# A four-layer mixture-of-experts kernel on one core: the order of mixed slots, a branch hint, a row add and a running count

## The chip, the cores and the metric

The kernel runs on one core of a Trainium2 chip. Times are device microseconds of one execution. The profile is of one execution, taken by the hardware profiler.

## The reference

The input is x of shape (2, 1024, 256), that is 2048 tokens of D = 256 channels in float32, with one conditioning row per sample. Four layers follow, each of the form `x = x + ffn(cond(x))`:

```python
x = x + L0_ffn(L0_cond(x, c, w), ...)      # modulated linear; shared SwiGLU + top-1 of 32 experts
x = x + L1_ffn(L1_cond(x, c, mask), ...)   # masked attention with 16 heads; attention with gated experts
x = x + L2_ffn(L2_cond(x, c, ...), ...)    # shared + top-2 of 8 GELU experts; shared + top-2 of 8 SwiGLU experts
x = x + L3_ffn(L3_cond(x, c, ...), ...)    # shared + top-2 of 8; top-1 of 16 experts with capacity
```

For this change four pieces matter. In layer 0's FFN each token goes to the one expert with the largest logit. In layer 1, for the mask that these inputs have, the layer's contribution is the same row for all tokens of a sample, so that it is added to every token as a bias. Layer 2's FFN is, per token and for each of its two experts,

```python
out_e = (silu(x @ w1_e) * (x @ w3_e)) @ w2_e      # w1_e, w3_e: 256 x 1024, w2_e: 1024 x 256
```

The token's result is a weighted sum of those two, to which a shared expert is added.

## The kernel before

All tensors of the tokens lie in SBUF, once with tokens on the partitions (Xt, Ht) and once with channels on them (XT, HT). Routed experts work on slots: 128 rows, gathered through DRAM (xbuf), each slot with one expert. Weights are loaded by SP's queue into `ring`, an SBUF buffer of 20 pieces of 1024 columns, parts of which a stage holds for its own sets of weights. A load is issued when the code names it, and waits for the last reader of the columns that it overwrites; SP's queue is in order. A reader that is recorded in the code after a load waits for that load. All engines run their instructions in the order that the scheduler gives them, and the helper `_behind(k, a, b)` puts instruction a behind b on its engine.

**Layer 2's FFN** (`_layer2_ffn`, about 590 to 1062 us). There are 39 ordinary slots and two mixed ones, numbered 39 and 40. An ordinary slot takes W1, W3 and W2 of one expert, 1 MB each, from set 0 or set 1 in the ring. A mixed slot has rows of three experts, in quarters of 32 rows: rows 0 to 63 from the first, 64 to 95 from the second, 96 to 127 from the third. Its experts lie in sets 0, 1 and 2 (set 2 is XT and acc, which are free there); for the second mixed slot in sets 2, 0 and 1. `slots(ids)` at L2320 goes through them in the order 39, 0 to 29, 40, 30, and then, under a branch that is not taken here, the rest. Slot 0, which follows slot 39, loads into set 0; slot 30, which follows slot 40, loads into set 1.

`Series.slot` (L1938) runs one slot against its neighbours on PE. It fetches rows of the slot after next, calls `weights()` for the loads and `products(...)` for the generator of the slot's matmuls, turns the next slot's rows to channel-major (`turn`, ps_cm at L500), stages the first part of its own matmuls, and then calls `close()`, which stages the last part of the slot before and sends its rows out (`put`). Then come the other parts. For an ordinary slot (`_ffn_products`) the parts are fpg and fpu for the first 512 hidden channels (16 matmuls each, then Silu on ACT as fsg and the product fa on DVE at L1996), fpg and fpu for the second 512, and in close() fpo (L2000). For a mixed slot (`_mixed_products`, L2010) the parts are mpg for both halves, mpu for both halves (L2031), the four transposes of the first half (mpt, L2021, with a copy maT on DVE and one on ACT at L2023), and in close() the transposes of the second half and then 32 matmuls mpo (L2044), which read W2 of the three experts.

**Layer 0** (up to 282 us). `_route_static` (L771), called from `lead` in the first hidden block of the shared expert, turns each token's expert into a row number. From the one-hot tensor l_oh (128 partitions, 16 token tiles, 32 experts) 16 adds on DVE, each needing the one before, make running counts l_cum over the tiles (L783). Two matmuls into l_R follow: l_oh against `before` (L786), and l_cum against ones (L789), then l_cnt (L792). Ranks and bases are sums over experts on DVE. The row numbers drive 15 row scatters on POOL, with one more later, and the slots' rows `xs` are fetched after the last. 24 slots follow (`Split.slot`): each stages fpg, fpu, then fpo of the slot before, then the transposes. The loop calls `ahead` after each for the next weights. After the loop `mark_branch_hint_location('rare', ...)`, placed behind the last slot's up product (`split.up`), puts a hint for PE on the branch 'rare' (L751), which decides on rare cases, among them overfull experts. For these inputs the Else side runs, with `_layer1_one`.

**Layer 1** (`_layer1_one`, 282 to 335 us). The layer's row is worked out for both samples by small matmuls. `col` holds it with channels on the partitions; rb is its copy for the matmuls s_pbi against layer 2's W1 and W3, which give the biases that layer 2 would get from the row. bi is s_pbi's copy, half by ACT and half by DVE; s_pbt turns it, and k.l2b holds it. At the end eight adds put `col` on XT: four token blocks of 512 by two channel halves, one on DVE and seven on ACT (L1321), the last six behind ACT's bi copy. Then comes layer 2's first shared product (spg, L1716).

Of the kernel before, what the change touches and what calls it, by code (L numbers as in the profile page):

```python
# [9 lines left out]
F32 = mybir.dt.float32  # L10
# [3 lines left out]
BF16 = mybir.dt.bfloat16  # L14
AF = mybir.ActivationFunctionType
ALU = mybir.AluOpType
AX = mybir.AxisListType
# [3 lines left out]
P = 128  # L21
# [5 lines left out]
NT = N // P  # L27
TB = 512
NB = N // TB
# [50 lines left out]
def _bc(ap, axis, shape):  # L80
    return ap.unsqueeze(axis).to_broadcast(shape)
# [104 lines left out]
def _one_hot(k, pool, ixf, n, E, name, tag=None):  # L186
    oh = pool.tile([P, NT, E], F32, name=name, tag=tag or name)
    k.nc.vector.tensor_tensor(oh, _bc(k.iota[:, 0:E], 1, [P, NT, E]),
                              ixf[:, :, n:n + 1].to_broadcast([P, NT, E]), ALU.is_equal)
    return oh  # L190
# [334 lines left out]
def _layer0(k):  # L525
    nc, A, XT, HT, Xt, Ht = k.nc, k.A, k.XT, k.HT, k.Xt, k.Ht
# [3 lines left out]
    NS = E * C // T  # L530
# [32 lines left out]
    with ExitStack() as ctx:  # L563
# [100 lines left out]
        for i in range(NS):  # L664
# [10 lines left out]
            next(pre, None)  # L675

            ahead(3 * (i * T // C), slots.load)
        with k.tc.issue_after(split.up.ins):
            k.tc.mark_branch_hint_location('rare', 'LikelyTaken', [mybir.EngineType.PE])
        assert next(pre, pre) is pre and not todo  # L680
        rare = k.pre.tile([1, 1], F32, name="l0_raref")
        nc.vector.tensor_tensor(rare, k.differf[0:1, :], end[0:1, E - 1:E], ALU.add)
# [90 lines left out]
def _route_static(k, pool, keep, psum, ixf, E, C, nov, name, ref):  # L773

    nc = k.nc
    K = -(-(N - C) // P)
    oh = _one_hot(k, pool, ixf, 0, E, name + "_oh", "s_oh")
    cum = pool.tile([P, NT + 1, E], F32, name=name + "_cum", tag="s_cum")  # L780
    nc.vector.memset(cum[:, 0, :], 0.0)
    for t in range(NT):
        nc.vector.tensor_add(cum[:, t + 1, :], cum[:, t, :], oh[:, t, :])  # L783
    R = psum.tile([P, NT, E], F32, name=name + "_R", tag="mm")

    i = nc.tensor.matmul(R.rearrange("p t e -> p (t e)"), k.before,  # L786
                         oh.rearrange("p t e -> p (t e)"), start=True, stop=False)
    _behind(k, i, ref)
    nc.tensor.matmul(R.rearrange("p t e -> p (t e)"), k.ones,  # L789
                     cum[:, 0:NT, :].rearrange("p t e -> p (t e)"), start=False, stop=True)  # L790
    cnt = psum.tile([P, E], F32, name=name + "_cnt", tag="mm")
    nc.tensor.matmul(cnt, k.ones, cum[:, NT, :], start=True, stop=True)  # L792
    w = pool.tile([P, NT, E], F32, name=name + "_w", tag="rt")
    nc.vector.tensor_mul(w, oh, R)
    r = pool.tile([P, NT], F32, name=name + "_rank", tag="s_rank")
    nc.vector.tensor_reduce(r, w, AX.X, ALU.add)
    cs = pool.tile([P, E], F32, name=name + "_cs", tag="s_cs")
    nc.vector.tensor_copy(cs, cnt)
    thr = pool.tile([P, K], F32, name=name + "_thr", tag="s_thr")
    nc.vector.tensor_scalar(thr, k.iota[:, 0:K], float(P), float(C), ALU.mult, ALU.add)  # L800
    over = pool.tile([P, E, K], F32, name=name + "_over", tag="rt")
    nc.vector.tensor_tensor(over, _bc(cs, 2, [P, E, K]), _bc(thr, 1, [P, E, K]), ALU.is_gt)
    nt = pool.tile([P, E], F32, name=name + "_nt", tag="s_nt")
    nc.vector.tensor_reduce(nt, over, AX.X, ALU.add)
    end = pool.tile([P, E], F32, name=name + "_end", tag="s_end")
    nc.vector.tensor_tensor_scan(end, k.ones[:, 0:E], nt, 0.0, ALU.mult, ALU.add)
    base = pool.tile([P, E], F32, name=name + "_base", tag="s_base")
    nc.vector.tensor_sub(base, end, nt)
    w2 = pool.tile([P, NT, E], F32, name=name + "_w2", tag="rt")
    nc.vector.tensor_tensor(w2, oh, _bc(base, 1, [P, NT, E]), ALU.mult)  # L810
    b = pool.tile([P, NT], F32, name=name + "_b", tag="s_b")
    nc.vector.tensor_reduce(b, w2, AX.X, ALU.add)

    nc.vector.tensor_scalar(b, b, float(P), float((E - 1) * C), ALU.mult, ALU.add)
    e = pool.tile([P, NT], F32, name=name + "_e", tag="s_e")
    nc.vector.tensor_scalar_mul(e, ixf[:, :, 0], float(C))
    ge = pool.tile([P, NT], F32, name=name + "_ge", tag="s_ge")
    nc.vector.tensor_single_scalar(ge, r, float(C), ALU.is_ge)
    nc.vector.tensor_tensor(b, b, e, ALU.subtract)
    nc.vector.tensor_mul(b, b, ge)  # L820
    nc.vector.tensor_tensor(b, b, e, ALU.add)
    nc.vector.tensor_tensor(r, r, b, ALU.add)
    rows = keep.tile([P, NT], U32, name=name + "_rows", tag="s_rows")
    nc.vector.tensor_copy(rows, r)
    done = pool.tile([1, nov, E], F32, name=name + "_done", tag="rt")
    nc.vector.tensor_tensor(done, _bc(end[0:1, :], 1, [1, nov, E]),
                            _bc(k.iota[0:1, 0:nov], 2, [1, nov, E]), ALU.is_le)
    ef = pool.tile([1, nov], F32, name=name + "_ef", tag="s_ef")
    nc.vector.tensor_reduce(ef, done, AX.X, ALU.add)
    nc.vector.tensor_scalar_min(ef, ef, float(E - 1))  # L830
    eid = keep.tile([1, nov], I32, name=name + "_eid", tag="s_eid")
    nc.vector.tensor_copy(eid, ef)
    n = keep.tile([1, 1], I32, name=name + "_nov", tag="s_nov")
    nc.vector.tensor_copy(n, end[0:1, E - 1:E])
    return rows, eid, n, end
# [191 lines left out]
def _layer1_one(k, psum, last):  # L1027
# [17 lines left out]
    def fill(n=1):  # L1045

        nonlocal last
        for _ in range(n):
            i = next(ahead, None)
            if i is not None:  # L1050
                pe(i)
            elif last is not None:
                last = _warm(k, psum, last, 2, tag="o", bufs=2)

    with ExitStack() as ctx:
# [237 lines left out]
        nc.vector.tensor_copy(rb[:, :, 0:2], pc)  # L1293
        nc.vector.tensor_copy(col, pc)
        fill()

        W1, W3, _ = k.l2
        pbi = psum.tile([P, TB], F32, name="s_pbi", tag="mm")
# [2 lines left out]
                pe(nc.tensor.matmul(pbi[quad[g], :], rb[:, c, :], (W1, W3)[g // 2][:, c, (g % 2) * TB:(g % 2 + 1) * TB],  # L1301
                                    start=c == 0, stop=c == 1, skip_group_check=True))
        bi = pool.tile([P, TB], F32, name="s_bi")
        copied = nc.scalar.copy(bi[:, 0:256], pbi[:, 0:256])
        nc.vector.tensor_copy(bi[:, 256:TB], pbi[:, 256:TB])
        pb = psum.tile([P, 2, D], F32, name="s_pb", tag="t", bufs=2)
        for b in range(2):
            pe(nc.tensor.matmul(pb[:, b, :], ab[:, b, :], row, start=True, stop=True))
# [3 lines left out]
            pe(nc.tensor.transpose(pbt[:, j, :], bi[:, j * P:(j + 1) * P], k.ident))  # L1312
        nc.vector.tensor_copy(k.l2b, pbt.rearrange("p j (g r) -> p j g r", g=4)[:, :, :, 0:2])
        nc.scalar.copy(rows, pb)
        for g in range(NB):
            for c in range(2):
                x = XT[:, c, g * TB:(g + 1) * TB]
                if g == c == 0:
                    nc.vector.tensor_scalar_add(x, x, col[:, c, 0:1])
                else:  # L1320
                    i = nc.scalar.activation(x, x, AF.Identity, bias=col[:, c, g // 2:g // 2 + 1])  # L1321
                    if g:
                        _behind(k, i, copied)
        assert next(ahead, None) is None


# [311 lines left out]
def _behind(k, inst, ref):  # L1638

    k.tc.add_manual_dep(inst.ins, ref.ins.name,  # L1640
                        mybir.DependencyInfo(mybir.DependencyClass.NoSync,
                                             mybir.DependencyReason.SCHED_ONLY))
# [266 lines left out]
class Series:  # L1909
# [3 lines left out]

    def __init__(self, k, slots, ids):
        self.k, self.slots, self.ids = k, slots, list(ids)
        self.xT, self.last, self.old = {}, None, None
        self.fetch(0)
        self.fetch(1)
        self.turn(0)
# [15 lines left out]
            self.xT[i] = self.slots.rows(i, made)  # L1935
            self.stage(made)

    def slot(self, i, products, weights):  # L1938

        n = self.ids.index(i)  # L1940
        self.fetch(n + 2)
        p = products(self.xT.pop(i), *weights())
        self.turn(n + 1)
        self.stage(next(p))
        self.close()
        part = next(p)
        while part is not None:
            self.stage(part)
            self.part = part
            part = next(p)  # L1950
        self.old = i, p
# [300 lines left out]
def _layer2_ffn(k):  # L2252
# [64 lines left out]
    def mixed(m, *to):  # L2317
        return [_expert_load(k, mid, 3 * m + q, sets[j], E) for q, j in enumerate(to) if j is not None]

    def slots(ids):  # L2320
        series = Series(k, by, ids)
        for n, i in enumerate(ids):
            if i == NS:
                series.slot(i, _mixed_products(k, pool, psum), lambda: mixed(0, 0, 1, 2))
            elif i > NS:
                series.slot(i, _mixed_products(k, pool, psum), lambda: [ahead[0], *mixed(1, None, 0, 1)])
            else:
                series.slot(i, _ffn_products(k, pool, psum, 2), lambda: weights(i))
            if i == 8:
                ahead = mixed(1, 2)  # L2330
            if i == MOST - 1:
                with k.tc.issue_after(series.part[len(series.part) // 2].ins):
                    k.tc.mark_branch_hint_location('l2f', 'LikelyTaken', [mybir.EngineType.PE])
        series.close()
# [551 lines left out]
```

## Time and profile before

| what | value |
|---|---|
| median of 3 runs | 1409.55 us (1408.58 to 1412.58) |
| the profiled execution's own time | 1411.02 us |
| its span | 1409.3 us |
| mean granted TensorE clock | 0.992 |
| PE busy | 1364.5 us, 97% of the span |
| DVE, ACT, POOL busy | 459.5, 304.3, 272.7 us |
| DMA, all queues | 265.25 MB, mean 188 GB/s |

The page divides the span into 40 slices; PE's busy share is nine tenths or more in nearly all of them. The waits view lists, for each engine, what it waited for with the time in total, the number of times and the longest. The timeline gives runs of equal instructions of an engine with start, length and the idle time ahead of them. The windows view gives busy time, clock and DMA traffic for any stretch. What is named behind an arrow is the instruction whose end is nearest to the end of the wait, which need not be what the instruction was waiting for.

### The profile page before, as it was taken

The page shows a single profiled execution, that of the slowest core. Times are in us where ns is not written, and L with a number is a line of the kernel's source. Part 1 is how long each engine was busy: PE and PEld are TensorE (multiplying, and loading weights), DVE is VectorE, ACT ScalarE, POOL GpSimd, SP SyncE. Part 2 cuts the span into 40 slices and gives each one's busy share as a digit, 9 for nine tenths or more (in the row PEclk, how much of TensorE's full clock was granted, in tenths as well). Part 3 has the DMA queues.
Part 4 walks back from the last instruction along what each step waited for, and adds up shares of the span by engine and source line. Part 5 has one row for each costly group of instructions (what it writes and reads, how often), then busy time and mean ns, then how long its engine had stood idle before and what let it go on. Part 6 is the DMA issues. An engine that isn't in the chain of part 4 may idle for free. (4 is left out here: it accounts for less than half of the span.)

```text
span 1409.3 us, 23114 instructions
## 1 busy us (share of the span) xinstructions
PE 1364.5 (97%) x8431; PEld 958.7 (68%) x8431; DVE 459.5 (33%) x1528; ACT 304.3 (22%) x640; POOL 272.7 (19%) x308
## 2 busy tenths in 40 slices
PE   9999999998999999999899999999999999998997
PEld 4544444654657876555599999999966557875675
DVE  4523322324413444511211111111114423458432
ACT  3212221234112112211111111111112212127121
POOL 0410001300432430053000000010000074430441
PEclk9999999999999999999999999999999999999899
DMA  9879992943312852092284456266447347748670
GB/s 313 308 238 342 357 368 84 302 90 135 113 53 80 249 188 81 1 334 70 81 309 157 152 197 222 78 209 225 149 156 256 122 158 233 244 148 280 206 230 16
DMA packets 185423, 265.25 MB, mean 188 GB/s; under 512 B 16759, under 2 KB 134655, under 8 KB 185296
## 3 DMA queue, kind: packets, MB, share of 16 engines
q1 hardware_dynamic: 163984, 221.65, 48.4%
q0 software_dynamic: 13744, 36.63, 7.3%
q10 hardware_dynamic: 7568, 5.34, 1.2%
q8 instruction: 71, 1.16, 0.3%
q14 instruction: 56, 0.46, 0.1%
HBM read 283.67 MB, written 46.82 MB: 235 GB/s over the span
## 5 line engine op out<-in xcount | busy, mean ns | idle before, releaser
L402 POOL DMA_INDIRECT tbuf<-ys,sdst x105 | 103.3, 984 | 467.0 <-ACT ys L2003 295.4
L1669 PE MATMUL spo<-ring,sa 128*128 128x256 f32 x704 | 164.9, 380 | 0.6 <-DVE sa L1697 0.4
L1669 PEld LDWEIGHTS spo<-ring,sa 128*128 128x128 f32 x704 | 132.8, 190 | 45.8 <-issue 28.9
L1697 DVE TENSOR_TENSOR sa<-ssg,spu 128x512 f32<-128x512 f32 x88 | 60.4, 686 | 241.5 <-PE spu L1684 232.8
L1996 DVE TENSOR_TENSOR fa<-fsg,fpu 128x512 f32<-128x512 f32 x62 | 42.6, 688 | 286.0 <-PE fpu L1991 286.0
L1991 PE MATMUL fpu<-xsT,ring 128*128 128x128 f32 x992 | 122.8, 278 | 5.3 <-SPq L2338 2.9
L1991 PE MATMUL fpg<-xsT,ring 128*128 128x128 f32 x992 | 121.1, 276 | 0.9 <-ACT maT L2023 0.9
L1991 PEld LDWEIGHTS fpu<-xsT,ring 128*128 128x128 f32 x992 | 117.4, 195 | 5.7 <-issue 5.7
L1991 PEld LDWEIGHTS fpg<-xsT,ring 128*128 128x128 f32 x992 | 117.9, 192 | 3.4 <-ACT maT L2023 1.1
L2000 PE MATMUL fpo<-ring,fa 128*128 128x256 f32 x496 | 112.3, 380 | 0.0
L1693 ACT ACTIVATE ssg<-spg 128x512 f32<-128x512 f32 x88 | 52.5, 597 | 267.8 <-PE spg L1684 261.5
L2000 PEld LDWEIGHTS fpo<-ring,fa 128*128 128x128 f32 x496 | 92.1, 191 | 11.8 <-issue 0.8
L1684 PE MATMUL spg<-HT,ring 128*128 128x512 f32 x192 | 92.1, 594 | 3.1 <-issue 2.4
L1684 PE MATMUL spu<-HT,ring 128*128 128x512 f32 x192 | 90.2, 593 | 0.0
L1967 PE MATMUL cph<-xsT,ring 128*128 128x128 f32 x576 | 77.5, 278 | 6.0 <-DMA ring<-in_L_r 4.3
L1684 PE MATMUL spg<-XT,ring 128*128 128x512 f32 x160 | 75.6, 594 | 1.3 <-PEq L2214 1.2
L1967 PEld LDWEIGHTS cph<-xsT,ring 128*128 128x128 f32 x576 | 70.1, 192 | 9.1 <-DVE sn L1893 3.7
L1684 PE MATMUL spu<-XT,ring 128*128 128x512 f32 x160 | 75.4, 593 | 0.0
L1974 PE MATMUL cpo<-ring,ch 128*128 128x256 f32 x288 | 73.8, 380 | 0.0
L1995 ACT ACTIVATE fsg<-fpg 128x512 f32<-128x512 f32 x62 | 37.0, 597 | 139.9 <-PE fpg L1991 139.9
L1684 PEld LDWEIGHTS spu<-HT,ring 128*128 128x128 f32 x192 | 36.3, 190 | 44.4 <-issue 43.9
L1889 DVE COPY xsT<-ps_cm 128x256 f32<-128x256 f32 x129 | 53.8, 417 | 31.2 <-PE ps_cm L500 31.1
(675 smaller groups left out, 1770.5 us busy)
## 6 DMA issues: line engine op xcount, KB each, us to landing
ring<-in_L_w SPq DMA_DIRECT2D x105, 1024.0 KB
ring<-in_L_r SPq DMA_DIRECT2D x72, 512.0 KB
ring<-in_L_r SPq DMA_DIRECT2D x144, 256.0 KB
xs<-xbuf SPq DMA_DIRECT2D x129, 129.0 KB
ring<-in_L_W SPq DMA_DIRECT2D x32, 512.0 KB
yt<-tbuf SPq DMA_DIRECT2D x48, 256.0 KB
XT<-in_L_r SPq DMA_DIRECT2D x16, 512.0 KB
HT<-in_L_r SPq DMA_DIRECT2D x8, 512.0 KB
```

The costliest lines, as they stand in the source:

```text
L402: i = k.nc.gpsimd.indirect_dma_start(out=self.ap, out_offset=bass.IndirectOffsetOnAxis(ap=idx, axis=0), in_=rows, in_offset=None, **end)
L1669: mm = nc.tensor.matmul(po[g // 2][:, g % 2, :], a[:, g * P:(g + 1) * P], W2[:, f, :], start=f == 0 and g % 2 == 0, stop=f == nf - 1, skip ...
L1684: mm = nc.tensor.matmul(ps, W[:, c, f * P:(f + 1) * P], X[:, c, cols], start=c == 0, stop=c == 1)
L1693: k.silu = nc.scalar.activation(sg, pg, AF.Silu)
L1697: mul = nc.vector.tensor_mul(a, sg, pu)
L1889: turned = nc.vector.tensor_copy(xT, _channel_major(k, self.psum, xs, made=made))
L1967: made = [nc.tensor.matmul(ph[:, f, :], R1[:, c, f * P:(f + 1) * P], xT[:, c, :], start=c == 0, stop=c == 1) for f in range(2) for c in ra ...
L1974: made = [nc.tensor.matmul(po, h[:, f, :], R2[:, f, :], start=f == 0, stop=f == 1) for f in range(2)]
L1991: made = [nc.tensor.matmul(ps[:, j, :], W[:, c, (f0 + j) * P:(f0 + j + 1) * P], xT[:, c, :], start=c == 0, stop=c == 1) for ps, W in ((pg, ...
L1995: nc.scalar.activation(sg, pg, AF.Silu)
L1996: nc.vector.tensor_mul(a[:, f0:f0 + 4, :], sg, pu)
L2000: made = [nc.tensor.matmul(po, a[:, f, :], W2[:, f, :], start=f == 0, stop=f == 4 * nh - 1) for f in range(4 * nh)]
```

## The change

There are four parts.

1. The branch hint of layer 0 is placed behind the up product of slot NS − 3 = 21, not of the last, 23.
2. `_route_static` has its one-hot tensor with the tiles innermost, with a zero column ahead of each expert's 16 tiles. One scan over 32 x 17 elements, `state = row * state + M`, with row 0 at each expert's start and 1 elsewhere, makes the running counts. `row` lies in the last two token tiles of Xr as bfloat16. The matmuls read the same tensors in the new order (l_R is expert by tile), and the two sums over experts read with a stride.
3. `_layer1_one` adds `col` to XT ahead of the s_pbi matmuls, five of the eight adds on DVE and three (the second channel half of blocks 0 to 2) on ACT, each engine's own in order; the bi copies come behind them.
4. A slot can be marked `soon`, which both mixed slots are. The slot after it then calls `close()` ahead of its own first part, not behind it. `weights()` and `turn` come ahead of that, as before.

```diff
--- before.py
+++ after.py
@@ -675,8 +675,9 @@
             next(pre, None)
 
             ahead(3 * (i * T // C), slots.load)
-        with k.tc.issue_after(split.up.ins):
-            k.tc.mark_branch_hint_location('rare', 'LikelyTaken', [mybir.EngineType.PE])
+            if i == NS - 3:
+                with k.tc.issue_after(split.up.ins):
+                    k.tc.mark_branch_hint_location('rare', 'LikelyTaken', [mybir.EngineType.PE])
         assert next(pre, pre) is pre and not todo
         rare = k.pre.tile([1, 1], F32, name="l0_raref")
         nc.vector.tensor_tensor(rare, k.differf[0:1, :], end[0:1, E - 1:E], ALU.add)
@@ -776,24 +777,28 @@
 
     nc = k.nc
     K = -(-(N - C) // P)
-    oh = _one_hot(k, pool, ixf, 0, E, name + "_oh", "s_oh")
-    cum = pool.tile([P, NT + 1, E], F32, name=name + "_cum", tag="s_cum")
-    nc.vector.memset(cum[:, 0, :], 0.0)
-    for t in range(NT):
-        nc.vector.tensor_add(cum[:, t + 1, :], cum[:, t, :], oh[:, t, :])
-    R = psum.tile([P, NT, E], F32, name=name + "_R", tag="mm")
-
-    i = nc.tensor.matmul(R.rearrange("p t e -> p (t e)"), k.before,
-                         oh.rearrange("p t e -> p (t e)"), start=True, stop=False)
+    M = pool.tile([P, E, NT + 1], F32, name=name + "_oh", tag="s_oh")
+    row = k.Xr[:, NT - 2:, :].rearrange("p t d -> p (t d)").bitcast(BF16)[:, 0:E * (NT + 1)]
+    row = row.rearrange("p (e t) -> p e t", e=E)
+    nc.vector.memset(row, 1.0)
+    nc.vector.memset(row[:, :, 0:1], 0.0)
+    nc.vector.memset(M[:, :, 0:1], 0.0)
+    oh = M[:, :, 1:]
+    nc.vector.tensor_tensor(oh, _bc(k.iota[:, 0:E], 2, [P, E, NT]), _bc(ixf[:, :, 0], 1, [P, E, NT]), ALU.is_equal)
+    cum = pool.tile([P, E, NT + 1], F32, name=name + "_cum", tag="s_cum")
+    nc.vector.tensor_tensor_scan(cum.rearrange("p e t -> p (e t)"), row.rearrange("p e t -> p (e t)"),
+                                 M.rearrange("p e t -> p (e t)"), 0.0, ALU.mult, ALU.add)
+    R = psum.tile([P, E, NT], F32, name=name + "_R", tag="mm")
+
+    i = nc.tensor.matmul(R, k.before, oh, start=True, stop=False)
     _behind(k, i, ref)
-    nc.tensor.matmul(R.rearrange("p t e -> p (t e)"), k.ones,
-                     cum[:, 0:NT, :].rearrange("p t e -> p (t e)"), start=False, stop=True)
+    nc.tensor.matmul(R, k.ones, cum[:, :, 0:NT], start=False, stop=True)
     cnt = psum.tile([P, E], F32, name=name + "_cnt", tag="mm")
-    nc.tensor.matmul(cnt, k.ones, cum[:, NT, :], start=True, stop=True)
-    w = pool.tile([P, NT, E], F32, name=name + "_w", tag="rt")
+    nc.tensor.matmul(cnt, k.ones, cum[:, :, NT], start=True, stop=True)
+    w = pool.tile([P, E, NT], F32, name=name + "_w", tag="rt")
     nc.vector.tensor_mul(w, oh, R)
     r = pool.tile([P, NT], F32, name=name + "_rank", tag="s_rank")
-    nc.vector.tensor_reduce(r, w, AX.X, ALU.add)
+    nc.vector.tensor_reduce(r, w.rearrange("p e t -> p t e"), AX.X, ALU.add)
     cs = pool.tile([P, E], F32, name=name + "_cs", tag="s_cs")
     nc.vector.tensor_copy(cs, cnt)
     thr = pool.tile([P, K], F32, name=name + "_thr", tag="s_thr")
@@ -806,10 +811,10 @@
     nc.vector.tensor_tensor_scan(end, k.ones[:, 0:E], nt, 0.0, ALU.mult, ALU.add)
     base = pool.tile([P, E], F32, name=name + "_base", tag="s_base")
     nc.vector.tensor_sub(base, end, nt)
-    w2 = pool.tile([P, NT, E], F32, name=name + "_w2", tag="rt")
-    nc.vector.tensor_tensor(w2, oh, _bc(base, 1, [P, NT, E]), ALU.mult)
+    w2 = pool.tile([P, E, NT], F32, name=name + "_w2", tag="rt")
+    nc.vector.tensor_tensor(w2, oh, _bc(base, 2, [P, E, NT]), ALU.mult)
     b = pool.tile([P, NT], F32, name=name + "_b", tag="s_b")
-    nc.vector.tensor_reduce(b, w2, AX.X, ALU.add)
+    nc.vector.tensor_reduce(b, w2.rearrange("p e t -> p t e"), AX.X, ALU.add)
 
     nc.vector.tensor_scalar(b, b, float(P), float((E - 1) * C), ALU.mult, ALU.add)
     e = pool.tile([P, NT], F32, name=name + "_e", tag="s_e")
@@ -1293,6 +1298,17 @@
         nc.vector.tensor_copy(rb[:, :, 0:2], pc)
         nc.vector.tensor_copy(col, pc)
         fill()
+        added = {}
+        for g in range(NB):
+            for c in range(2):
+                x, by, one = XT[:, c, g * TB:(g + 1) * TB], col[:, c, g // 2:g // 2 + 1], c == 1 and g < 3
+                if one:
+                    i = nc.scalar.activation(x, x, AF.Identity, bias=by)
+                else:
+                    i = nc.vector.tensor_scalar_add(x, x, by)
+                if one in added:
+                    _behind(k, i, added[one])
+                added[one] = i
 
         W1, W3, _ = k.l2
         pbi = psum.tile([P, TB], F32, name="s_pbi", tag="mm")
@@ -1301,8 +1317,8 @@
                 pe(nc.tensor.matmul(pbi[quad[g], :], rb[:, c, :], (W1, W3)[g // 2][:, c, (g % 2) * TB:(g % 2 + 1) * TB],
                                     start=c == 0, stop=c == 1, skip_group_check=True))
         bi = pool.tile([P, TB], F32, name="s_bi")
-        copied = nc.scalar.copy(bi[:, 0:256], pbi[:, 0:256])
-        nc.vector.tensor_copy(bi[:, 256:TB], pbi[:, 256:TB])
+        _behind(k, nc.scalar.copy(bi[:, 0:256], pbi[:, 0:256]), added[True])
+        _behind(k, nc.vector.tensor_copy(bi[:, 256:TB], pbi[:, 256:TB]), added[False])
         pb = psum.tile([P, 2, D], F32, name="s_pb", tag="t", bufs=2)
         for b in range(2):
             pe(nc.tensor.matmul(pb[:, b, :], ab[:, b, :], row, start=True, stop=True))
@@ -1312,15 +1328,6 @@
             pe(nc.tensor.transpose(pbt[:, j, :], bi[:, j * P:(j + 1) * P], k.ident))
         nc.vector.tensor_copy(k.l2b, pbt.rearrange("p j (g r) -> p j g r", g=4)[:, :, :, 0:2])
         nc.scalar.copy(rows, pb)
-        for g in range(NB):
-            for c in range(2):
-                x = XT[:, c, g * TB:(g + 1) * TB]
-                if g == c == 0:
-                    nc.vector.tensor_scalar_add(x, x, col[:, c, 0:1])
-                else:
-                    i = nc.scalar.activation(x, x, AF.Identity, bias=col[:, c, g // 2:g // 2 + 1])
-                    if g:
-                        _behind(k, i, copied)
         assert next(ahead, None) is None
 
 
@@ -1913,7 +1920,7 @@
 
     def __init__(self, k, slots, ids):
         self.k, self.slots, self.ids = k, slots, list(ids)
-        self.xT, self.last, self.old = {}, None, None
+        self.xT, self.last, self.old, self.soon = {}, None, None, False
         self.fetch(0)
         self.fetch(1)
         self.turn(0)
@@ -1935,14 +1942,17 @@
             self.xT[i] = self.slots.rows(i, made)
             self.stage(made)
 
-    def slot(self, i, products, weights):
+    def slot(self, i, products, weights, soon=False):
 
         n = self.ids.index(i)
         self.fetch(n + 2)
         p = products(self.xT.pop(i), *weights())
         self.turn(n + 1)
+        if self.soon:
+            self.close()
         self.stage(next(p))
         self.close()
+        self.soon = soon
         part = next(p)
         while part is not None:
             self.stage(part)
@@ -2321,9 +2331,10 @@
         series = Series(k, by, ids)
         for n, i in enumerate(ids):
             if i == NS:
-                series.slot(i, _mixed_products(k, pool, psum), lambda: mixed(0, 0, 1, 2))
+                series.slot(i, _mixed_products(k, pool, psum), lambda: mixed(0, 0, 1, 2), True)
             elif i > NS:
-                series.slot(i, _mixed_products(k, pool, psum), lambda: [ahead[0], *mixed(1, None, 0, 1)])
+                series.slot(i, _mixed_products(k, pool, psum), lambda: [ahead[0], *mixed(1, None, 0, 1)],
+                            True)
             else:
                 series.slot(i, _ffn_products(k, pool, psum, 2), lambda: weights(i))
             if i == 8:
```

## The prediction

> **What bounds the kernel.** I read the page first. The span is 1409.3 us, the profiled execution's own time 1411.02 us (1.7 us lie around the span), the median of the runs 1409.55 us. I add my terms to 1411.02 and then take off 1.47 us to come to the median.
>
> ```profile
> span 1409.3 us, 23114 instructions
> PE 1364.5 (97%) x8431; PEld 958.7 (68%) x8431; DVE 459.5 (33%) x1528; ACT 304.3 (22%) x640; POOL 272.7 (19%) x308
> ```
>
> PE is busy for 97%: only about 45 us of the span are without a matmul. So an edit is worth what it does to PE's idle time, to the number of PE's instructions (unchanged here) and to PE's clock. The second view is therefore the list of PE's waits (us in total, times, longest):
>
> ```profile
> PE fpu L1991 <- SPq L2338: 2.9, 1, 2.9
> PE spg L1716 <- ACT XT L1321: 2.7, 1, 2.7
> PE spg L1684 <- issue: 2.4, 1, 2.4
> PE fpu L1991 <- DMA ring<-in_L_w: 2.4, 1, 2.4
> PE l_R L789 <- DVE l_cum L783: 1.1, 1, 1.1
> PE fpg L1991 <- ACT maT L2023: 0.9, 1, 0.9
> PE mpo L2044 <- DVE fa L1996: 0.5, 1, 0.5
> ```
>
> All four edits meet here: lines 1, 4, 6 and 7 are the slots that follow the two mixed slots of layer 2, line 2 is layer 1's row add, line 3 the branch behind layer 0, line 5 layer 0's counts. If everything vanished, 12.9 us would go.
>
> **Mixed slots, the decisive part.** The third view is PE's timeline behind mixed slot 0 (start, us, instruction, in brackets the idle time before it):
>
> ```profile
> 698.88 0.66 PE L2021 MATMUL mpt<-ident,ma 128*128 128x128 f32 x4
> 699.38 0.38 PE L500 MATMUL ps_cm<-ident,xs 128*128 128x128 f32 x2
> 700.65 2.02 PE L1991 MATMUL fpg<-xsT,ring 128*128 128x128 f32 x16 [0.89 <-ACT maT L2023]
> 705.06 2.02 PE L1991 MATMUL fpu<-xsT,ring 128*128 128x128 f32 x16 [2.39 <-DMA ring<-in_L_w]
> 706.92 0.60 PE L2021 MATMUL mpt<-ident,ma 128*128 128x128 f32 x4
> 708.01 0.42 PE L2044 MATMUL mpo<-ring,maT 128*32 128x256 f32 x3 [0.49 <-DVE fa L1996]
> ```
>
> SP's queue issues six loads of 1 MB in this time: slot 0's W1 at 695.54, W3 at 698.97, W2 at 699.57, then slot 1's W1 at 700.10 and W3 at 700.80. The sixth, slot 1's W2, waits 9.2 us for mpo. From 700 to 712 us the DMA engines move 4.2 MB at a mean of 350 GB/s, so that the loads land one behind the other: W1 lets fpg start at 700.65, W3 lets fpu start at 705.06. The same ring columns hold the mixed slot's W2 and slot 0's W2, and weights() is called ahead of close(), in both kernels. In the instruction list the first mpo therefore waits for slot 0's W2 load, in both. The DVE copy that its bracket goes by had been over since 700.16 us; what ended the 0.49 us can only be that landing, at about 708.0. Before, fpg and fpu of slot 0 fill the time until then. After, mpt and mpo stand ahead of them: mpt is ready, mpo is not, and fpg, whose W1 is there at 700.65, queues behind it on PE, which is in order.
>
> So PE ends its second mpt at about 700.3 and idles until 708.0: 7.7 us in place of 0.89 + 2.39 + 0.49 = 3.77. mpo takes 3.6 us (to 711.60). Before, fpg of the second half starts at 711.60; after, fpg and fpu of the first half must still run, 3.7 us (such a pair goes from 1054.30 to 1057.97 in slot 30). **+3.7 us.** If W2 lands as early as W3 did (705.1), it is +0.8; later than 708.0 it can't be.
>
> Mixed slot 1 is alike: W3 and W2 of slot 30 are issued at 1040.27 and 1040.9, and mpo reads the columns that this W2 fills. Before, fpu starts at 1045.53 and fpo at 1057.97. DMA traffic ends in the slice 1047 to 1048, so W2 lands at about 1048.0 (not before W3, 1045.5; not after mpo's start, 1050.06). After: idle from about 1041.6 to 1048.0, mpo 3.6, two pairs 7.3, so fpo at 1058.9 at full clock.
>
> **The clock.** The windows view (PE, PEld, DVE, ACT, POOL busy, then the granted clock, DMA share, GB/s):
>
> ```profile
> 1043.00:1044.00 1.00, 0.00 (x0) 0.00 (x0) 0.00 (x0) 0.27 (x1) 0.00 (x0) 1.00 1.07 442
> 1045.00:1046.00 1.00, 0.47 (x2) 0.51 (x3) 0.00 (x0) 0.00 (x0) 0.00 (x0) 0.50 1.09 381
> 1047.00:1048.00 1.00, 1.00 (x6) 1.00 (x6) 0.00 (x0) 0.00 (x0) 0.00 (x0) 0.50 0.60 188
> 1051.00:1052.00 1.00, 1.00 (x20) 0.54 (x16) 0.00 (x0) 0.00 (x0) 0.00 (x0) 0.79 0.00 0
> ```
>
> An idle time of 2.95 us is followed here by 6.8 us at a granted 0.50 (1044.4 to 1051.2): fpu takes 3.75 us in place of 1.95. Idle times of 2.39, 2.45 and 2.75 us (the lines above) were not followed by any, one of 2.15 us ahead of 1310.85 was: length alone does not decide. The three other spells, from 1290 to 1318 us, last 3.3, 3.7 and 6.8 us. With 7.7 and 6.4 us of idle time I expect a spell behind both, of 3.3 to 6.8 us, part of which falls into the idle time itself; work lost is half of it, 1.7 to 3.4 us, and I take 2.6 each. With it slot 0 is late by 3.7 + 2.6 = **6.3 us** (0.8 to 7.1), and slot 30's fpo starts at 1061.5 in place of 1057.97: **+3.5 us** (with W2 at 1045.5 and no loss −1.6; with 1050.06 and 3.4 us lost +6.4). Both together: +9.8.
>
> [...]
>
> **The row add of layer 1.** PE's first matmul of layer 2 waits 2.75 us (332.80 to 335.55) for the last of seven ACT adds (0.64 us each, the last four 332.94 to 335.50). The adds now stand ahead of the bi copies, while PE still does pbi (until 330.87): three on ACT from 328.87, 3 x 0.64, to 330.8, and five on DVE. The only DVE add took 0.49 us and overlaps its neighbours; at 0.43 to 0.49 each they end at 331.1 to 331.3. ACT's bi copy started at 330.97 and DVE's at 331.37, so neither is pushed, and pbt is on time. The wait shrinks to what PE needs for its start, 0 to 0.4 us: **−2.5 us** (0 to −2.75; 0 if DVE's adds push bi and pbt by as much as they save). What is late next is the l2b copy at 333.03, not needed by spg.
>
> **Layer 0's counts.** 16 DVE adds (36.26 to 40.1) become one scan of 128x544. The nearest rows are the scans 128x32, 0.224 us, and 128x136, 0.442 us: 2.1 ns per element, so 1.3 us, to 37.6. PE's first l_R ends at 37.70; its waits of 1.11 us ahead of L789 and 0.41 us in the transposes that stand in between go, or part of them. The two reduces read with a stride now, at 0.36 in place of 0.27 us for 128x128, so 0.2 to 0.4 us each for four times the elements is given back on the way to the row numbers; the memsets lie in idle time. The later chain (15 row scatters on POOL, the last at 74.93, SP's fetch of xs at 77.70) ends in a wait of 0.86 us for xs at 79.99, where what PE gained can be lost again if that chain starts no earlier. **−0.8 us** (+0.8 to −1.5).
>
> **The branch hint.** PE waits 2.45 us behind the branch (236.53, "issue"). On DVE, which has no hint, the same branch costs 3.0 us; on PE in layer 2, with a hint 5.1 us ahead of its branch, 0.63 us. Here the hint runs at 226.4, 6.8 us ahead of the branch at 233.2, and helps little. After, it is about 13 us earlier, at about 213 us, where DMA traffic falls from over 90% to quiet. Either it helps now, −1.8 us, or lead was not what it lacked, 0. Nearer lies 0, since 5.1 us were enough elsewhere: **−0.3 us**.
>
> **The sum**: +9.8 − 2.5 − 0.8 − 0.3 = +6.2; 1411.0 + 6.2 = 1417.2, less 1.47 is **1415.7 us**. By the lower bounds of all terms −0.8 − 2.75 − 1.5 − 1.8 = −6.9, 1402.7; by the upper +13.5 + 0 + 0.8 + 0 = +14.3, 1423.8.
>
> **Rivals.** (B) *The wait is there, but cheap*: W2 lands nearly with W3, or the clock holds. Without any loss of clock the slots are 3.7 + 0.9 = +4.6, less 3.6 for the other edits: 1410.5; with W2 landing early as well, down to 1402.7. For it: 2.75 us idle at 332.80 left the clock alone. Against: the new idle times are twice as long.
> (C), on the other side: *mpo doesn't wait for the next slot's W2.* mpt and mpo fill the time in which PE waits for W1 and W3: 0.6 + 3.6 = 4.2 us of work, against 3.77 us of waiting behind slot 0, all of which goes; behind slot 30 the 2.95 us go and the clock never falls (2.9 us). That is −9.6 −3.6: 1396.3 us. It decides if mpo starts by about 701 us. For it: the waits view names DVE for the 0.49 us, not a DMA. Against: the DVE copy was long done.
> (D) *Edits that do nothing*: hint without effect, counts swallowed at xs: 1416.8, within the forecast's own range.
>
> **Chances.** Forecast with D, 1411 to 1422: 0.60. B, 1402 to 1411: 0.24. C: 0.13. Above 1422: 0.03. The range 1402 to 1422 leaves out 0.16. A measurement of this kernel can tell about 0.3% (4.2 us) from no change: faster (under 1405.3) C and 0.05 of B, 0.18; the same (to 1413.8) 0.26; slower 0.56.
>
> **What will show it.** PE's waits after: an entry of 5 to 8 us ahead of mpo, twice, and none ahead of fpu; windows at 0.50 behind each. spg L1716's wait under 0.5 us. No wait at l_R. The first spg behind the branch: 2.45 or 0.6 us. Wrong if mpo starts within 2 us of its mpt, if the clock stays at 1.00 behind 7 us of idle time, or if DVE's adds end later than 331.4.

## The result, and the profile after

The changed kernel takes 1414.72 us at the median of 13 runs (1412.53 to 1418.48), the kernel before 1409.55 us at the median of as many beside it (1405.56 to 1413.83). The ratio is 1.0036, with a 95% interval of 1.0023 to 1.0049: the change makes the kernel slower by 3 to 7 us. The forecast was +6.2 us, 1415.7 us. The profiled execution took 1413.27 us, its span is 1411.6 us.

The page of the changed kernel, first two lines, and then its list of PE's waits (engine, line, what ended the wait; us in total, times, longest):

```profile
span 1411.6 us, 23099 instructions
...
PE 1364.6 (97%) x8431; PEld 955.5 (68%) x8431; DVE 461.1 (33%) x1519; ACT 302.3 (21%) x636; POOL 273.3 (19%) x308
```

```profile
PE mpo L2054 <- DMA ring<-in_L_w: 6.7, 1, 6.7
PE mpo L2054 <- SPq L2349: 6.6, 1, 6.6
...
PE spg L1691 <- issue: 2.2, 1, 2.2
...
PE ps_cm L500 <- DMA xs<-xbuf: 0.7, 2, 0.5
```

PE has as many instructions as before and is busy as long. Of the seven waits that were shown of the kernel before, those ahead of fpg and fpu (0.9, 2.4, 2.9 us), of l_R (1.1) and of layer 2's first spg (2.7) are gone, but for 0.17 us at l_R and 0.43 us at spg. In their place stand two waits ahead of mpo, 6.7 and 6.6 us. The branch's wait, 2.2 us, has stayed.

PE's timeline of the changed kernel behind mixed slot 0 (lines of mpo left out):

```profile
694.80 0.66 PE L2031 MATMUL mpt<-ident,ma 128*128 128x128 f32 x4
695.30 0.38 PE L500 MATMUL ps_cm<-ident,xs 128*128 128x128 f32 x2
695.79 0.66 PE L2031 MATMUL mpt<-ident,ma 128*128 128x128 f32 x4
703.16 0.65 PE L2054 MATMUL mpo<-ring,maT 128*32 128x256 f32 x3 [6.71 <-DMA ring<-in_L_w]
...
709.46 2.05 PE L2001 MATMUL fpg<-xsT,ring 128*128 128x128 f32 x16
711.34 1.95 PE L2001 MATMUL fpu<-xsT,ring 128*128 128x128 f32 x16
713.13 1.95 PE L2001 MATMUL fpg<-xsT,ring 128*128 128x128 f32 x16
```

The first and last of these have their counterparts before in the line at 698.88, which the prediction shows, and in this one:

```profile
711.60 2.05 PE L1991 MATMUL fpg<-xsT,ring 128*128 128x128 f32 x16
```

mpt starts 4.08 us earlier than before (694.80 for 698.88), fpg of slot 0's second half 1.53 us later (713.13 for 711.60): the slot has lost 5.61 us. One mpo takes 0.65 us here and 0.42 us before. The windows view says why (the clock is the third figure from the end):

```profile
697.00:698.00 1.00, 0.00 (x0) 0.00 (x0) 0.00 (x0) 0.32 (x1) 0.00 (x0) 1.00 1.01 414
699.00:700.00 1.00, 0.00 (x0) 0.00 (x0) 0.00 (x0) 0.00 (x0) 0.00 (x0) 0.50 0.98 349
...
706.00:707.00 1.00, 1.00 (x13) 0.47 (x9) 0.00 (x0) 0.00 (x0) 0.00 (x0) 0.50 1.07 418
...
709.00:710.00 1.00, 1.00 (x16) 0.59 (x9) 0.00 (x0) 0.34 (x1) 0.00 (x0) 1.00 0.01 3
```

PE is idle from 696.45; the granted clock falls at about 698.5 and comes back at about 708.7, when mpo is nearly done. Behind mixed slot 1 it is the same: idle until 1050.34, the clock at 0.50 from about 1046.6 to 1053.4, fpo of slot 30 at 1062.66 in place of 1057.97. The lines of mpo and fpo after, and that of fpo before:

```profile
1050.34 0.63 PE L2054 MATMUL mpo<-ring,maT 128*32 128x256 f32 x1 [6.60 <-SPq L2349]
1062.66 3.62 PE L2010 MATMUL fpo<-ring,fa 128*128 128x256 f32 x16
```

```profile
1057.97 3.62 PE L2000 MATMUL fpo<-ring,fa 128*128 128x256 f32 x16
```

By landmarks on PE in the two traces: the slots of layer 0 start 1.36 us earlier (first fpg 79.56 for 80.92), the first spg behind the branch 1.63 us earlier (234.90 for 236.53), layer 2's first spg 3.78 us earlier (331.77 for 335.55), slot 30's fpo 4.69 us later. The two lines of spg, before and after:

```profile
335.55 1.98 PE L1716 MATMUL spg<-XT,ring 128*128 128x512 f32 x4 [2.75 <-ACT XT L1321]
```

```profile
331.77 1.95 PE L1723 MATMUL spg<-XT,ring 128*128 128x512 f32 x4 [0.43 <-PE s_pbt L1328]
```

At the end of the span 2.3 us are left. Between slot 30's fpo and that end no line of the change runs; before idled 1.5 us more there (ahead of ps_bk and cph, above all) and had one spell of 3.4 us at 0.50 more. I take this for chance of single executions: over 13 runs each the difference is 5.2 us.

### The profile page after: what moved, and what is told of

It is laid out like the page before. It is cut to its first block, busy times and chain, and to the rows that moved or that the text cites. A ratio compares the mean times of both kernels' runs of the same rounds, so it can differ in the third digit from the quotient of the medians.

```text
span 1411.6 us, 23099 instructions
## 1 busy us (share of the span) xinstructions
PE 1364.6 (97%) x8431; PEld 955.5 (68%) x8431; DVE 461.1 (33%) x1519; ACT 302.3 (21%) x636; POOL 273.3 (19%) x308
```

## Experiments

**The mixed slots alone, and the rest alone.** All times are set against the kernel before on the same chip. e1 is the kernel before, with part 4 of the change and nothing else:

```diff
         self.turn(n + 1)
+        if self.soon:
+            self.close()
         self.stage(next(p))
```

> The kernel before with part 4 alone (close() of a mixed slot ahead of the next slot's first part, still behind its weights()). Theory (mpo waits for the next slot's W2 load, and the idle time halves the clock): in the trace after, slot 0's second fpg is late by 5.6 us more than its mpt, and slot 30's fpo by 3.3 us more, so +8.9 us against before, a ratio of 1.0063 (1.0045 to 1.0080); two idle times of 6 to 7.5 us ahead of mpo. Rival (the two slots cost little, and the 5.2 us of the change come from another part or from layer 3's spells of the clock): under +4 us, ratio below 1.003.

Measured: 1418.58 us for 1408.17, ratio 1.0085 (1.0071 to 1.0099). The two waits ahead of mpo are 6.71 and 6.25 us, and the first spg behind the slots is reached 7.96 us later in the trace (1070.19 for 1062.23). The interval says 10 to 14 us, more than the trace and than the 8.9 us that I expected, and the ratio lies a little above the expected range; the rival is out. Where the 8.9 us fell short is taken up below, in point 3 of why the prediction was right.

e2 is the changed kernel without part 4; its core:

```diff
-        if self.soon:
-            self.close()
```

> The changed kernel without part 4. Theory: the other three parts give in full what the trace after shows up to layer 2's first spg, 331.77 in place of 335.55, so -3.8 us against before, ratio 0.9973 (0.996 to 0.9985); waits ahead of fpu and mpo as before. Rival (what PE gains early is taken back at later waits for DMA, as cph's): 0 to -1.5 us, ratio 0.999 to 1.000.

Measured: 1403.84 us for 1408.17, ratio 0.9967 (0.9956 to 0.9978). The other three parts keep what they gain. Against this the whole change is 1.0036 / 0.9967 = 1.0069, some 9.7 us (7 to 12 by the two intervals), slower through part 4 alone: the forecast's term was +9.8.

**What mpo waits for.** If it waits for the next slot's W2 because that load is recorded ahead of it, then closing ahead of the loads must take the wait away. e3 is the changed kernel with this edit:

```diff
-        p = products(self.xT.pop(i), *weights())
-        self.turn(n + 1)
         if self.soon:
             self.close()
+        p = products(self.xT.pop(i), *weights())
+        self.turn(n + 1)
```

> The changed kernel, with close() ahead of weights() for a slot behind a mixed one, so that the next slot's W2 load waits for mpo and not mpo for it. Theory: PE waits under 1 us ahead of mpo, fpg and fpu find W1 and W3 landed, the clock stays at 1.00 in both places: -3.8 -9.2 = -13 us against before, up to 3 us less if slot 1's loads, now behind mpo, come late; ratio 0.991 (0.990 to 0.9945). Rival (the loads themselves are the limit there, whatever the order: 5 MB at 350 to 400 GB/s): PE waits the same 4 to 7 us somewhere in slot 0 or slot 1, -3.8 us or less, ratio 0.997 or above.

Measured: 1398.81 us for 1408.17, ratio 0.9942 (0.9928 to 0.9955), faster than both kernels, at the small end of what was expected. From PE's timeline of e3 (32 mpo and a ps_cm between the first two lines are left out):

```profile
695.45 0.66 PE L2031 MATMUL mpt<-ident,ma 128*128 128x128 f32 x4 [0.31 <-DVE ma L2048]
...
699.90 1.95 PE L2001 MATMUL fpg<-xsT,ring 128*128 128x128 f32 x16
701.69 1.95 PE L2001 MATMUL fpu<-xsT,ring 128*128 128x128 f32 x16
...
708.40 2.02 PE L2001 MATMUL fpg<-xsT,ring 128*128 128x128 f32 x16 [0.97 <-DVE sn L1900]
711.01 2.02 PE L2001 MATMUL fpu<-xsT,ring 128*128 128x128 f32 x16 [0.59 <-DMA ring<-in_L_w]
```

mpo waits for nothing in both places, slot 0 finds its weights, and no slice shows a clock under 1.00 there. What is left are 0.97 and 0.59 us ahead of slot 1's products at 708.40 and 711.01. Now SP's queue holds slot 0's W2 until mpo is done (699.73), and slot 1's loads stand behind it. The wait ahead of the first spg behind slot 30 has grown too, to 1.46 us from 0.63 before.

In both kernels mpo reads what the *next* slot's W2 load has put into the columns, and in e3 what the mixed slot's own load did. For the drawn inputs this is the same matrix: by the reference the experts of this layer get 315, 532, 766, 431, 654, 388, 375 and 635 rows, so that slot 39's first expert is expert 0, as slot 0's is, and slot 40 has no third expert: its rows 96 to 127 are empty. For other counts it need not be so; then only an order as in e3, W2's load behind close(), has mpo read its own weights. Behind slot 39 PE waited 6.7 us for a second copy of weights that were there, behind slot 40 6.6 us for weights of rows that are empty.

e9 is e3, with slot 0's W1 and W3, and then slot 1's, issued ahead of close(). weights() of the slot behind a mixed one is a generator there; its first step issues those four loads, its second slot 0's W2:

```diff
+        w = weights()
         if self.soon:
+            early = next(w)
             self.close()
-        p = products(self.xT.pop(i), *weights())
+            w = early + next(w)
+        p = products(self.xT.pop(i), *w)
```

> As e3, but of slot 0's loads only W2 comes behind close(), and slot 1's W1 and W3 are issued ahead of it, so that they need not wait for mpo on SP's queue. Theory (what e3 still loses at 708.4 and 711.0, 0.97 and 0.59 us, is the three loads that queue behind the one that waits for mpo): both waits go, 1.5 us less than e3: ratio to before 0.993 (0.9915 to 0.9945), no idle time over 0.4 us from 694 to 720. Rival (six loads in 12 us are the limit of the DMA engines, so that a wait comes back at slot 0's fpu or fpo or slot 1's fpu): as e3, 0.994 to 0.9955.

Measured: 1412.92 us where the kernel before took 1423.7 us (another chip), ratio 0.9926 (0.9910 to 0.9941), the fastest version. The timeline shows no idle time from 697 to 724 us: both waits are gone. Between e3 and e9 the intervals overlap, so that in time the further gain is not shown, only in the trace.

**The clock.** Does the idle time halve it, or the DMA traffic of 350 to 420 GB/s that goes on meanwhile? e4 is the changed kernel with 14 filling matmuls, e5 with 30:

```diff
         made = turn(1)
+        w = psum.tile([P, F], F32, name="fill", tag="mm")
+        made += [nc.tensor.matmul(w.rearrange("p (j q) -> p j q", q=P), k.ident16, _bc(k.ident16, 1, [P, 4, P]),
+                                  start=True, stop=True, skip_group_check=True) for _ in range(14)]
```

> The changed kernel with 14 bf16 matmuls of 128x512 (0.43 us each, into a tile that nobody reads) between the second mpt and mpo, which keep PE busy while it waits for W2. Theory (the idle time itself halves the clock): mpo starts as late as before, but at 1.00; 2.7 us less behind slot 39 and 1.7 us less behind slot 40 than in the changed kernel, so 1410.3 us, ratio to before 1.0005 (0.9985 to 1.002). Rival (the half clock comes from the DMA traffic or from elsewhere): the spells at 0.50 stay, ratio 1.0035 to 1.005.

Measured: 1414.12 us for 1408.17, ratio 1.0045 (1.0032 to 1.0059). It told nothing: a filler takes some 0.21 us and not 0.43 when they run one behind another (30 take 6.64 us in e5; 0.43 us is the distance from start to start of the float32 matmuls of this width in before, as mpu's at 695.31 and 695.74), so 3.73 and 3.47 us of idle time stayed ahead of mpo and the clock still fell, to 0.50 from about 702.7 on, for 3.4 us behind slot 39 and 6.8 us behind slot 40.

> As e4, with 30 of the filling matmuls in place of 14: in e4 the 14 took 3.2 us, 3.7 and 3.5 us of idle time were left, and the clock still fell to 0.50, so that e4 could not tell the theories apart. At 0.21 us each 30 take 6.5 us and reach up to the landing of W2. Theory (idle time halves the clock): no slice under 0.9 from 694 to 710 and from 1040 to 1058, and 2.7 + 1.7 us less than the changed kernel's 1414.7: 1410.3, ratio to before 1.0005 to 1.002. Rival (the DMA traffic halves it): the spells stay, ratio 1.0035 to 1.005.

Measured: 1409.85 us for 1408.98, ratio 1.0008 (0.9998 to 1.0017). The fillers of e5 and its windows:

```profile
696.75 6.64 PE L2054 MATMUL fill<-ident 128*128 128x512 bf16 x30
703.64 0.42 PE L2057 MATMUL mpo<-ring,maT 128*32 128x256 f32 x3 [0.26 <-DMA ring<-in_L_w]
```

```profile
700.00:702.00 2.00, 2.00 (x11) 0.94 (x10) 0.00 (x0) 0.00 (x0) 0.00 (x0) 1.00 1.08 371
702.00:704.00 2.00, 1.74 (x15) 0.75 (x17) 0.00 (x0) 0.00 (x0) 0.00 (x0) 1.00 1.08 390
704.00:706.00 2.00, 2.00 (x44) 1.42 (x38) 0.00 (x0) 0.00 (x0) 0.00 (x0) 1.00 1.03 412
```

mpo starts as late as in the changed kernel (8.4 us behind its first mpt in both), under the same traffic, but at 0.42 us and a clock of 1.00. In this kernel the idle time of 6.7 and 6.6 us is what brings the clock to 0.50, and the halved clock was (1.0036 − 1.0008) x 1409 = 3.9 us of the change's cost (some 2 to 6 by the two intervals), 4.4 expected. The wait itself is the rest.

**The other three parts.** e6, e7 and e8 are the kernel before with part 3, part 2 and part 1 of the change, each alone, as in the diff of the change.

> The kernel before with part 3 alone. Theory: the wait ahead of layer 2's first spg falls from 2.75 to 0.43 us as in the trace after, and nothing takes it back: -2.3 us, ratio 0.9984 (0.997 to 0.9995). Rival (cph's waits for weights in layer 2's conditioning take it back): ratio 0.9995 to 1.0005.

Measured: 1406.85 us for 1408.98, ratio 0.9983 (0.9973 to 0.9994). The wait ahead of layer 2's first spg is 0.43 us.

> The kernel before with part 2 alone. Theory: the waits of 1.11 and 0.41 us at l_R and ps_tm go, xs's wait stays at 0.5 to 0.9 us, so the first slot's fpg starts 1.3 us earlier: -1.3 us, ratio 0.9991 (0.998 to 1.000). Rival (the wait for xs swallows it): first fpg of the slots as before within 0.4 us, ratio 0.9997 to 1.0005.

Measured: 1406.89 us for 1408.98, ratio 0.9989 (0.9978 to 1.0000). The waits for xs at the first slot are 0.60 and 0.63 us in place of 0.86, and the first fpg starts at 80.28 for 80.92. So here about half of the gain was swallowed, in the trace of the whole change nothing (its waits for xs are 0.74 us in all); the time can't tell. Single traces scatter here: on the chips of e1 to e8 the first fpg starts at 80.92, 80.91, 80.63 and 80.29 with the old counts (before, e1, e6, e8), at 79.56, 79.40, 79.37, 79.55, 79.59 and 80.28 with the new (the changed kernel, e2 to e5, e7), 1.1 us earlier in the mean.

> The kernel before with part 1 alone. Traces with the hint in its old place show the branch on PE at 3147 and 3092 ns, with the new place 2807, 3102, 2547 and 2537 ns. Theory: the place changes the branch by chance only or by 0.4 us at most: -0.3 us, ratio 0.9998 (0.999 to 1.0005). Rival (two slots earlier is what it lacked): 0.6 us of idle time ahead of the first spg, -1.8 us, ratio 0.9987.

Measured: 1408.93 us for 1408.98, ratio 1.0002 (0.9991 to 1.0013). The branch on PE takes 2957 ns.

e10 is the kernel before without the hint; in e11 the two lines stand in the loop, under `if i == NS // 2`:

```diff
-        with k.tc.issue_after(split.up.ins):
-            k.tc.mark_branch_hint_location('rare', 'LikelyTaken', [mybir.EngineType.PE])
```

> The kernel before without the branch hint of layer 0. Theory (the hint in either place leaves the branch at 2.5 to 3.1 us, so it does little): branch on PE 2.5 to 3.3 us, idle 1.8 to 2.6 us, ratio 1.000 (0.999 to 1.001). Rival (the hint does part of the fetch and the branch would be longer without it): branch above 3.5 us, ratio above 1.0005.

> The kernel before with the hint behind slot 12's up product, some 75 us ahead of the branch. One look at the branch on PE. Theory (lead is not what the hint lacks): 2.5 to 3.3 us, idle 1.8 to 2.6 us. Rival (the fetch needs longer under full DMA traffic): idle 0.6 us.

Measured: e10 1426.0 us for 1423.7, ratio 1.0018 (1.0006 to 1.0030); e11 1423.61 us in its one run. The branch as an instruction of PE's queue, in e10 and in e11 (ns three times, start in us):

```profile
L749 PEldq COMPARE_BRANCH  x1: 4082/4082/4082, 234.2 to 234.2; - x1
```

```profile
L752 PEldq COMPARE_BRANCH  x1: 2952/2952/2952, 234.6 to 234.6; - x1
```

Here my theory fell in half: the hint does something. Without it the branch takes 4.08 us and PE idles 3.38 us, about 1.1 us more than with it. The time says 2.6 us (0.9 to 4.3); in e10's trace the 3.38 us are followed by 6.8 us at a clock of 0.50, which may be the rest. But with the hint in the old place the branch took 3147, 3092, 2642 and 2667 ns in four traces, in the new place 2807, 3102, 2547, 2537, 2942, 2957 and 3067 ns in seven, and 2952 ns with a lead of 75 us. Lead is not what it lacks. What makes up the remaining 2.5 to 3.1 us, where layer 2's hinted branch cost 0.63 us of idle time in before, stays open.

## Why the prediction was right

1. *mpo must wait, since weights() stays ahead of close().* Right, shown by e3. The idle times were forecast at 7.7 and 6.4 us and are 6.7 and 6.6, the first 1.0 us too long. W2 landed at 703.2 in place of 703.9 (708.0 less the 4.1 us by which all is earlier); why it came 0.7 us sooner is not shown.
2. *The clock.* That both idle times would halve it was right, shown by e5; that the losses come so near the 2.6 us forecast for each is in part luck. The spells were put at 3.3 to 6.8 us; they last 10.2 us behind slot 39, of which 4.7 fall into the idle time, and 6.8 behind slot 40. (The spell of before ran from 1044.6 to 1051.4, not from 1044.4 to 1051.2, and the two short ones both last 3.4 us; the sums don't change.) Behind slot 39 mpo took 703.16 to 709.46, 6.3 us for 3.6: 2.7 us. Behind slot 40 it took 1050.34 to 1055.42, some 1.5 us too long. e5 gives 3.9 us for both in place of 5.2.
3. *Slots 0 and 30 late by 6.3 and 3.5 us.* 5.6 and 3.3 in the trace. In time 9.7 us by difference, 10 to 14 us by e1, for 9.8. The 3.3 are low, and so near the forecast because both start from the same trace of before, which lost 2.9 us to its own spell behind slot 40. From slot 40's first mpt to slot 30's fpo the seven traces without part 4 (before, e2, e6 to e8, e10, e11) take 15.9 to 17.8 us, before 17.84; the changed kernel and e1 take 21.1 and 22.0. From slot 39's first mpt to slot 0's second fpg the seven take 11.7 to 13.2 us, the two 18.3 and 17.1. By these means part 4 costs 5.4 and 4.8 us, 10.2 together, which fits both times.
4. *The row add, −2.5 us.* In the trace 3.78 − 1.63 = 2.15 us, in time −2.4 us. DVE's five adds took 2.07 us (2.2 to 2.4 reckoned), ACT's three 1.95, and they pushed neither copy.
5. *The counts, −0.8 us.* The scan took 1.29 us for 1.3. In the trace of the whole change the slots start 1.36 us earlier, in e7 0.64, in the mean of the traces above 1.1. I had missed that the one-hot write takes 1.09 us in the new layout in place of 0.69 (it ends at 37.17 and PE waits 0.17 us for it), and put the strided reduce at 0.2 to 0.4 us more: it is 1.03 for 0.69.
6. *The hint, −0.3 us.* Nothing that can be measured, e8.

The sum of the trace's terms up to slot 30 is −1.36 − 0.28 − 2.15 + 5.61 + 3.26 = +5.1 us against +6.2, and in time +5.2 (the stretches between gained 0.4 us more, hence the 4.69). Rival C (mpo doesn't wait) would have been 1396.3 us, 13 less than before; e3 and e9, in which it really doesn't, are 8 and 10 us below before by their ratios. Rival B (a wait without loss of clock) would have been 1410.5 us, 1.0 more than before; e5, which makes it so, is 1.1 above. Both had the wrong condition; B's price was right, C's some 3 to 5 us too low.

## What to carry to other kernels

When a step is moved ahead of another, look at which loads were recorded ahead of it, not only at its own inputs: a load into columns that it reads becomes its input, even where it brings the same data (6.7 and 6.6 us of waiting here, none in e3). A step that had other work in front of it may have been waiting all along, and the trace shows this only as half a microsecond (0.49 us ahead of mpo in before). And the idle times of 6.7 and 6.6 us on PE cost more than themselves here: the clock, at 0.50 behind both, added 1.5 to 2.7 us to each.

## What was not expected of the hardware

The clock fell 2.0 us after PE had gone idle behind slot 39 (696.45 to about 698.5) and about 2.9 us after it had behind slot 40 (1043.7 to 1046.6); in the kernel before an idle time of 2.75 us did nothing and one of 2.15 us did. The same wait need not have the same price. The one of 2.8 to 2.95 us ahead of slot 30's fpu is followed by 6.8 us at 0.50 in before and e8, by 3.4 us in e6 and e7, by none in e2. The one of 2.75 us ahead of layer 2's first spg is followed by none in before, e1 and e7, and by 3.4 us in e8:

```profile
334.72 3.40 PE L1717 MATMUL spg<-XT,ring 128*128 128x512 f32 x4 [2.75 <-ACT XT L1322]
```

In all thirteen traces a spell at 0.50 lasts 3.4, 6.8 or 10.2 us and nothing between, but for those that run into the end of the span. In e2 the 2.41 us at the branch were followed by such a spell as well, and layer 2's first spg came 1.6 us later than in the changed kernel (333.40 for 331.77), though nothing else differs up to there. So a single trace of this kernel is uncertain by up to some three microseconds (half of 6.8 us) wherever PE idles for about two or more: 2.15 us in before and 2.41 us in e2 were followed by a spell.

On the chip of e9 to e11 the kernel before took 1423.7 us, in place of 1408 to 1410 on the others. All three traces from it have a wait of 9.0 to 9.7 us in layer 3's shared products that no trace from the other chips has; in e9 ACT is without an instruction for 19.7 us there:

```profile
1145.09 1.09 ACT L1700 ACTIVATE ssg<-spg 128x512 f32<-128x512 f32 x2 [19.70 <-remote]
```

What held ACT was not tried. It is in all three kernels traced on that chip, and before, which was not traced there, takes some 14 us longer there too, so I take the ratios to stand.
